# Block 3's attention output by seven products, with norms, unpacking and the weighing of q placed elsewhere

## The chip, the cores and the metric

The kernel runs on one core of one Trainium2 chip. The metric is the device time of one execution in microseconds. TensorE (PE) multiplies, and its results land in PSUM banks. VectorE (DVE) and ScalarE (ACT) read those banks; GpSimd (POOL) works on SBUF alone. SyncE (SP) issues most of the DMAs. Each engine runs its own queue in order, and waits on semaphores of the others.

## The reference, cut to what matters

A two-layer network over 2 x 1024 rows of 512 floats: linear attention, an FFN with 4-bit weights, gated linear attention, and an FFN over picked rows, each with a residual and a layernorm. The change lies in the first part alone:

```python
q = _feature_map(proj(Wq))          # elu(x) + 1
k = _feature_map(proj(Wk))
v = proj(Wv)
kv = jnp.einsum('bhtd,bhte->bhde', k, v)
z = 1.0 / (jnp.einsum('bhtd,bhd->bht', q, k.sum(axis=2)) + 1e-06)
out = jnp.einsum('bhtd,bhde,bht->bhte', q, kv, z)
...
x = _layernorm(x + out @ Wo.T)
```

## The kernel before

The 2048 rows are four blocks of 512 rows (0 and 1 are the first sequence, 2 and 3 the second), each held as four tiles of 128 x 512. In the first stage, which ends at about 236 us, a sequence `b` has blocks `i = 2b` and `j = 2b + 1`. The projections k and q of a block are Strassen's products in Winograd's form (`by_seven`): seven products of four 128x256 matmuls in place of sixteen 128x512 ones, for which DVE forms sums of the operands (S1, S2, S3 in lines 398 to 415) and adds results up. `elu1` (ACT lines 345 and 346, then DVE line 347) makes the feature map. POOL sums the rows of k (`sum_k`, line 461, one addition per tile); `add_xk` multiplies x and k on PE (line 442). One matmul with ones spreads the sum of k over the partitions (`ksumb`, line 467, copied by ACT in line 468). `weigh` (lines 483 to 489, DVE alone) divides each q row by its dot product with that sum, in five instructions per tile. PE then turns q (`turned`, line 235, copied by ACT in line 551).

The attention's output is q times a 512x512 matrix G (`G_rows`). For blocks 0, 1 and 2, `o_products` makes it of seven products (line 565), whose results DVE adds to x at once (line 571). Two of the products' operands, S1 and S2, come from `q_sums` (lines 519 and 520), two more from lines 582 and 587. Its last step takes the block's row statistics on DVE (`row_stats`, lines 226 and 227) and normalises the block: the power on POOL (line 219), and four POOL instructions (line 221). Block 3's output is made tile by tile instead (`add_o`, line 610): four 128x512 matmuls, an addition to x (line 617) and the tile's statistics, with the turning of the next tile between.

The FFN's packed weights are unpacked in the background: `unpack_some(n)` takes n jobs, each a load on SP into one of two buffers (line 285), a shift and a mask on DVE (lines 288 and 289), and one or two copies on ACT (line 292). There are 16 jobs of 704 columns and 11 of 512.

The order is made by hand: `run` takes the steps of a list of products and, behind each, the other steps listed for it. `behind()` chains PE's instructions in that order, `tc.issue_after` puts an instruction behind another, and a scheduler orders what is free.

PSUM has eight banks. `acc_bank` takes banks 4 to 7 in turn, and the FFN stage takes its first banks by where that turn stands:

```python
last = turn_of["acc"]
y_banks = [4 + (last + i) % 4 for i in (2, 3, 0, 1)]
chunk_banks = [(2, 3), (0, 1), tuple(y_banks[2:])]
```

The FFN stage begins with three chunks side by side. Each step of a chunk is two 128x512 matmuls (line 942) into its `gatep` or `upp` bank, scaled in place by ACT (line 967) or DVE (line 969) ahead of the next step. Block 0's input for it is split into `x1Th` and `x1Tl` in lines 267 and 268. Some of these matmuls are scheduled between block 3's products.

Of the kernel before, what the change touches and what calls it, by code (L numbers as in the profile page):

```python
# [10 lines left out]
F32 = mybir.dt.float32  # L11
# [5 lines left out]
ALU = mybir.AluOpType  # L17
AX = mybir.AxisListType
# [3 lines left out]
P = 128  # L22
B, T, C = 2, 1024, 512
NB = 4
KC = C // P
# [48 lines left out]
def body(ctx: ExitStack, tc: tile.TileContext, a: dict, out: bass.AP):  # L74
    nc = tc.nc
# [5 lines left out]
    sp = ctx.enter_context(tc.tile_pool(name="small", bufs=3))  # L81
# [14 lines left out]
    def acc_bank(name):  # L96
        return bank("acc", name)
# [43 lines left out]
    x_t = [x[:, :, :C] for x in x_row]  # L141
# [22 lines left out]
    t, src = new_xT(0)  # L164
# [59 lines left out]
    def row_stats(mv, x):  # L224
        st = sp.tile([P, 6], F32, tag="st", name="st")
        nc.vector.bn_stats(st, x)  # L226
        nc.vector.bn_aggr(mv, st)
# [80 lines left out]
    anchor = [None]  # L308
# [49 lines left out]
    for _ in range(7):  # L358
        ins = nc.tensor.matmul(idle[:, :P], ones, ones, start=True, stop=True).ins
    last_pe = [ins]  # L360

    def behind():

        return ExitStack() if last_pe[0] is None else tc.issue_after(last_pe[0])
# [67 lines left out]
    pairs_of, mv_of, G_of, acc_of, ksum_of = {}, {}, {}, {}, {}  # L432
    tile_of = lambda i: slice(i * P, (i + 1) * P)
# [44 lines left out]
    def weigh(blk, t):  # L478

        for r in range(2):  # L480
            x = pairs_of["q", blk][t][:, r]
            e = wk.tile([P, C], F32, tag="e", name="qk")
            nc.vector.tensor_mul(e, x, ksum_of[blk // 2])
            z = sp.tile([P, 16], F32, tag="z", name="z", bufs=2)
            nc.vector.tensor_reduce(z, e.rearrange("p (h d) -> p h d", d=32), AX.X, ALU.add)
            nc.vector.tensor_scalar_add(z, z, 1e-6)
            nc.vector.reciprocal(z, z)
            x3 = x.rearrange("p (h d) -> p h d", d=32)
            weighed[0] = nc.vector.tensor_mul(x3, x3, z.unsqueeze(2).to_broadcast([P, 16, 32])).ins

    weighed = [None]
    vkm_of, qT, TG, o_of, parts = {}, {}, {}, {}, []

    def values(b):
# [58 lines left out]
    def o_products(blk):  # L553

        A11, A12, A21, A22 = (qT[blk][:, 2 * e : 2 * e + 2, 256 * t : 256 * t + 256] for t in range(2) for e in range(2))
        G = G_of[blk // 2]
        B11, _, B21, B22 = (G[:, 2 * e : 2 * e + 2, 256 * o : 256 * o + 256] for e in range(2) for o in range(2))
        T1, T2, T3, T4 = TG[blk // 2]

        def product(ps, a, b, first, t, o):  # L560

            with behind():
                for r in range(2):
                    for k in range(2):
                        ins = nc.tensor.matmul(
                            ps[:, 256 * r : 256 * r + 256], a[:, k, r * P : (r + 1) * P], b[:, k],
                            start=first and r == 0 and k == 0, stop=k == 1, skip_group_check=True,
                        ).ins
            last_pe[0] = ins
            x = x_t[blk][:, 2 * t : 2 * t + 2, 256 * o : 256 * o + 256]  # L570
            return nc.vector.tensor_add(x, x, ps.rearrange("p (r c) -> p r c", r=2)).ins

        if blk not in S_of:
            q_sums(blk)
        S1, S2 = S_of[blk]
        grow = acc_bank("grow")
        added = product(grow, A11, B11, True, 0, 0)
        with tc.issue_after(added):
            for rest in TG_rest:
                rest()  # L580
            TG_rest.clear()
            nc.vector.tensor_sub(A21, A11, A21)
        yield
        product(acc_bank("P2"), A12, B21, True, 0, 0)
        yield
        product(grow, S2, T2, False, 1, 0)
        nc.vector.tensor_sub(A12, A12, S2)
        yield
        side = acc_bank("P7")
        product(side, A21, T3, True, 1, 1)  # L590
        yield
        product(grow, S1, T1, False, 1, 1)
        yield
        product(side, A22, T4, False, 1, 0)
        yield
        product(grow, A12, B22, False, 0, 1)
        yield
        mv = mv_of[blk] = sp.tile([P, 4, 2], F32, tag="mv", name="mv")
        with tc.issue_after(weighed[0]):
            for i in range(4):  # L600
                row_stats(mv[:, i], x_t[blk][:, i])
            layernorm(x_t[blk], mv, by=nc.gpsimd)
        yield

    def add_o(blk, i):

        ao = acc_bank("ao")
        with behind():
            for k in range(KC):
                ins = nc.tensor.matmul(  # L610
                    ao, qT[blk][:, k, tile_of(i)], G_of[blk // 2][:, k], start=k == 0, stop=k == KC - 1
                ).ins
        last_pe[0] = ins
        x = x_t[blk][:, i]
        if i == 0:
            mv_of[blk] = sp.tile([P, 4, 2], F32, tag="mv", name="mv")
        nc.vector.tensor_add(x, ao, x)
        row_stats(mv_of[blk][:, i], x)

    def split_some(*part):  # L620
        if 0 in part:
# [10 lines left out]
    for k in range(KC):  # L632
        for i in range(4):
            for o in (slice(0, 256), slice(256, 512)) if k == 0 else (slice(0, 512),):
                with behind():
                    last_pe[0] = nc.tensor.matmul(
                        first[i][:, o], xT[0][:, k, tile_of(i)], Wk[:, k, o],
                        start=k == 0 and o.start == 0, stop=k == KC - 1, skip_group_check=True,
# [21 lines left out]
    def some_xk(blk, *part):  # L660
        return [lambda i=i: add_xk(blk, i) for i in part]

    def turns(blk, *part):
        return [lambda i=i: turned(blk, i) for i in part]

    def some_o(blk, n):

        def one():
            if blk not in o_of:
                o_of[blk] = o_products(blk)  # L670
            next(o_of[blk])

        return [one] * n

    def whole_o(*part):
        return [lambda i=i: add_o(3, i) for i in part]

    job = lambda n: [lambda: unpack_some(n)]

    def k_products(blk):  # L680
        return by_seven(xT[blk], Wk, Ts["k"], S_rooms, pairs_of.setdefault(("k", blk), []), lambda t: sum_k(blk, t))

    def q_products(blk, ready):
        return by_seven(xT[blk], Wq, Ts["q"], S_rooms, pairs_of.setdefault(("q", blk), []), ready)

    step = lambda f, *x: [lambda: f(*x)]
# [4 lines left out]
    for b in range(B):  # L691
        i, j = 2 * b, 2 * b + 1
        if b:
            run(
                k_products(i),
                turns(1, 0, 1) + job(1), job(1),
                turns(1, 2, 3) + some_o(1, 1) + job(1), some_o(1, 2) + job(1), some_o(1, 5) + job(1),
            )
        q_ready = [] if b else step(q_weights)
        run(  # L700
            k_products(j), [],
            some_xk(i, 0, 1) + job(2), some_xk(i, 2) + job(1) + q_ready, some_xk(i, 3) + job(1), job(1 + b),
        )
        if b == 0:
            Ts["q"] = sums_of_weights(Wq, slices(staged[0], 0, 3))
        else:

            Tq = place_w(1, "Tq")
            for n in range(3):
                nc.scalar.copy(Tq[:, n], staged[0][:, n])  # L710
            Ts["q"] = (*slices(Tq, 0, 2), Ts["q"][2], *slices(Tq, 2, 3))
            S_rooms[0] = pieces_of(Tq[:, 3])
        run(
            q_products(i, lambda t: weigh(i, t)), [],
            some_xk(j, 0, 1) + job(1 + b), some_xk(j, 2) + step(spread_ksum, b) + job(1), some_xk(j, 3) + job(1 + b),
        )
        if b == 0:
            xT[2] = load_xT(2)
        split = [step(split_some, n) if b else [] for n in range(4)]
        rings["free"] = (rings["sum"][(turn_of["sum"] + 1) % 2],)  # L720
        run(
            q_products(j, lambda t: None),
            step(values, b),
            turns(i, 0, 1) + split[0] + job(1 - b),
            turns(i, 2, 3) + split[1] + step(q_sums, i) + step(G_rows, b),
            some_o(i, 2) + split[2] + some_o(i, 1) + job(1 - b),
            step(all_free) + some_o(i, 1) + step(weigh, j, 0) + split[3] + some_o(i, 3) + step(weigh, j, 1) + some_o(i, 1)
            + job(1 - b),
        )
        if b == 0:  # L730
            xT[3] = load_xT(3)
    for more in (
        turns(3, 0, 1) + whole_o(0) + turns(3, 2) + whole_o(1) + turns(3, 3) + whole_o(2, 3)
    ):
        more()
    late = mv_of[3]
# [186 lines left out]
    with tc.tile_pool(name="s2", bufs=1) as wk2:  # L923
# [24 lines left out]
        class Chunk:  # L948
# [29 lines left out]
            def step(self, e, k, by):  # L978
                self.product(e, k)
                self.end(e, k, by)  # L980

        class Normed:
# [35 lines left out]
            def stats(self, i):  # L1018
                row_stats(self.mv[:, i], x_t[self.blk][:, i])

            def norm(self, i):
                norm_tiles(self.blk, self.mv, (i,))
# [588 lines left out]
    turns, last_hp = [0], [None]  # L1611
# [436 lines left out]
```

## Time and profile before

| | |
|---|---|
| time, three runs | 906.47, 905.47, 903.45 us; median 905.47 us |
| the profiled execution | 904.14 us, span 902.4 us |
| mean granted TensorE clock | 0.998 |
| PE busy | 881.0 us, 98% of the span |
| DVE, ACT, POOL busy | 686.4, 378.9 and 262.1 us |

The span runs from the first to the last instruction of the profiled execution, whose own time is 1.74 us longer. The profile counts a float32 matmul as two records, so "x8" of 128x256 is one product of four matmuls. A row's first two numbers in the timeline are its start and its length; where several like it follow each other, they are merged. "L571" is line 571 of the kernel. What stands in brackets at the end is the idle time before it and what ended it.

### The profile page before, as it was taken

What the parts mean: (1) busy time and instruction counts of PE and PEld (TensorE: products, weight loads), DVE (VectorE), ACT (ScalarE), POOL (GpSimd) and SP (SyncE); (2) the same over time, 40 slices, a digit from 0 to 9 for tenths busy, and PEclk for the clock granted to TensorE, in tenths of its full rate; (3) what the DMA queues carried; (4) which work ended last, traced back from release to release, by engine and by line L of the source; (5) the groups of instructions that cost most, each with busy time, mean ns of one, the idle gap of its engine ahead of it and who ended that gap; (6) DMA issues with size and microseconds to landing.
All of it is one profiled execution on the core that took longest, in us unless ns stands there. A gap on an engine that the chain in (4) does not pass through costs nothing. (4 is left out here: it accounts for less than half of the span.)

```text
span 902.4 us, 10909 instructions
## 1 busy us (share of the span) xinstructions
PE 881.0 (98%) x3923; PEld 687.5 (76%) x3923; DVE 686.4 (76%) x1320; ACT 378.9 (42%) x648; POOL 262.1 (29%) x229
## 2 busy tenths in 40 slices
PE   9999999999999999999999989999999999999996
PEld 5668886687688888888876767787585888888886
DVE  2569995589787797897878975858977976998535
ACT  2345343463477886986866233231201223220000
POOL 1020075200573456655654220020340030000112
PEclk9999999999999999999999999999999999999999
DMA  9632211201421404314003144000024220330001
GB/s 319 225 98 79 77 62 47 92 26 24 118 82 48 47 1 99 43 58 117 13 24 97 44 94 187 1 1 0 1 95 142 92 94 1 115 119 1 12 36 47
DMA packets 88007, 64.85 MB, mean 72 GB/s; under 512 B 63214, under 2 KB 63770, under 8 KB 87441
## 3 DMA queue, kind: packets, MB, share of 16 engines
q1 hardware_dynamic: 85313, 58.89, 22.4%
q0 software_dynamic: 1920, 4.22, 1.2%
q10 hardware_dynamic: 720, 1.05, 0.3%
q8 instruction: 31, 0.51, 0.2%
q14 instruction: 23, 0.19, 0.1%
HBM read 48.37 MB, written 17.88 MB: 73 GB/s over the span
## 5 line engine op out<-in xcount | busy, mean ns | idle before, releaser
L1001 DVE TENSOR_TENSOR yp<-yp,ratio 128x512 f32<-128x512 f32 x160 | 103.3, 692 | 17.2 <-PE yp L942 16.8
L219 POOL TENSOR_TENSOR rs<-rs,table 128x4 f32<-128x4 f32 (+1 forms) x19 | 17.2, 904 | 292.0 <-DVE rs L218 291.8
L967 ACT ACTIVATE gatep<-gatep,scale 128x512 f32<-128x512 f32 x132 | 83.8, 658 | 35.9 <-PE gatep L942 26.5
L942 PE MATMUL gatep<-x1Th,wgu 128*128 128x512 f32 x176 | 70.2, 399 | 0.0
L942 PE MATMUL yp<-wdn,hhi 128*128 128x512 f32 x176 | 70.1, 398 | 0.0
L942 PE MATMUL yp<-wdn,hlo 128*128 128x512 f32 x176 | 69.9, 397 | 0.2 <-POOL hlo L976 0.2
L942 PE MATMUL gatep<-x1Tl,wgu 128*128 128x512 f32 x176 | 69.3, 394 | 0.3 <-DVE x1Tl L268 0.3
L942 PE MATMUL upp<-x1Tl,wgu 128*128 128x512 f32 x176 | 68.8, 391 | 0.0
L942 PE MATMUL upp<-x1Th,wgu 128*128 128x512 f32 x176 | 68.8, 391 | 0.0
L967 ACT ACTIVATE upp<-upp,scale 128x512 f32<-128x512 f32 x100 | 64.8, 663 | 6.5 <-PE upp L942 3.0
L976 POOL TENSOR_TENSOR hlo<-whole,hhi 128x512 fp32r<-128x512 f32 x43 | 55.6, 1292 | 3.5
L975 POOL CAST hhi<-whole 128x512 fp32r<-128x512 f32 x43 | 26.3, 611 | 88.4 <-DVE whole L973 86.9
L973 DVE SCALAR_TENSOR_TENSOR whole<-upp,scale,silu 128x512 f32<-128x512 f32 x43 | 32.3, 750 | 19.5 <-PE upp L942 11.4
L910 PE MATMUL go<-spare,spare 128*128 128x256 f32 x192 | 44.0, 381 | 0.0
L442 PE MATMUL xk<-pair,x 128*128 128x512 f32 x96 | 42.7, 592 | 0.0
L226 DVE BATCH_NORM_STATS2 st<-x 128x6 f32<-128x512 f32 x64 | 42.2, 674 | 0.4
L910 PEld LDWEIGHTS go<-spare,spare 128*128 128x128 f32 x192 | 36.0, 190 | 6.7 <-issue 2.1
L942 PEld LDWEIGHTS yp<-wdn,hhi 128*128 128x128 f32 x176 | 33.0, 188 | 9.6 <-DVE yp L1001 1.1
L942 PEld LDWEIGHTS gatep<-x1Th,wgu 128*128 128x128 f32 x176 | 33.0, 188 | 9.1 <-ACT gatep L967 1.1
L942 PEld LDWEIGHTS gatep<-x1Tl,wgu 128*128 128x128 f32 x176 | 33.1, 188 | 8.2 <-DVE x1Tl L268 0.6
L942 PEld LDWEIGHTS yp<-wdn,hlo 128*128 128x128 f32 x176 | 33.1, 188 | 8.0 <-POOL hlo L976 0.6
L1364 POOL TENSOR_TENSOR sum<-sum,sq 128x512 f32<-128x512 f32 x12 | 17.6, 1466 | 73.9 <-issue 63.9
(469 smaller groups left out, 2083.3 us busy)
## 6 DMA issues: line engine op xcount, KB each, us to landing
pk<-in_gu SPq DMA_DIRECT2D x16, 352.0 KB, 3.7
x<-in_x SPq DMA_DIRECT2D x4, 1024.0 KB, 14.1
w<-in_w SPq DMA_DIRECT2D x1, 4096.0 KB, 13.6
xs<-picked SPq DMA_DIRECT2D x4, 1024.0 KB, 4.9
out<-x SPq DMA_DIRECT2D x4, 1024.0 KB, 4.4
w<-in_w SPq DMA_DIRECT2D x4, 1024.0 KB, 7.4
x0T<-in_xT SPq DMA_DIRECT2D x3, 1024.0 KB, 7.5
x1r<-x SPq DMA_DIRECT2D x3, 1024.0 KB, 5.1
```

Source lines behind the costliest of these rows:

```text
L219: power = nc.gpsimd.tensor_tensor(rs[:, :n], rs[:, :n], const("mhalf")[:, :n], ALU.pow).ins
L226: nc.vector.bn_stats(st, x)
L442: ins = nc.tensor.matmul(acc_of[b][c], x_t[blk][:, i, c * P : (c + 1) * P], pairs_of["k", blk][i // 2][:, i % 2], start=blk % 2 == 0 and i ...
L910: ins = nc.tensor.matmul(ps[:, 256 * m : 256 * m + 256], w[:, k, m], b[:, k, 256 * half : 256 * half + 256], start=first and m == 0 and k ...
L942: nc.tensor.matmul(ps, w, x, start=start and n == 0, stop=stop and n == 1, skip_group_check=True)
L967: nc.scalar.activation(ps, ps, AF.Copy, scale=s)
L973: nc.vector.scalar_tensor_tensor(self.whole, ps, s, self.silu, ALU.mult, ALU.mult)
L975: nc.gpsimd.tensor_copy(hi, self.whole)
L976: nc.gpsimd.tensor_sub(lo, self.whole, hi.bitcast(F32))
L1001: nc.vector.tensor_tensor(self.y[:, i] if g == NI - 1 else ps, ps, ratio[:, g], ALU.mult)
L1364: nc.gpsimd.tensor_add(sum2, sum2, sq)
```

## The change

`o_products` also makes block 3's output, so `add_o` and `whole_o` go; block 3's four tiles of q are turned first, then come the seven products, then the statistics of its four tiles (`stats`). The end of `o_products` becomes a function `norm`, called for block 0 beside the last k products of block 3, for block 1 beside the q products of block 2, for block 2 where it was. Unpacking jobs beside the k products of block 2 fall from five to one, and rise from six to nine beside block 3's k products and from five to six beside block 2's q products. The weighing of q of blocks 1 and 3 is put behind the last two additions to x that precede it, and its second half is moved by one product.

```diff
-            weighed[0] = nc.vector.tensor_mul(x3, x3, z.unsqueeze(2).to_broadcast([P, 16, 32])).ins
-
-    weighed = [None]
+            with tc.issue_after(adds[-2 + r]) if blk % 2 else contextlib.nullcontext():
+                nc.vector.tensor_mul(e, x, ksum_of[blk // 2])
+                ...
+                weighed[0] = nc.vector.tensor_mul(x3, x3, z.unsqueeze(2).to_broadcast([P, 16, 32])).ins
+
+    weighed, adds = [None], []
...
-            return nc.vector.tensor_add(x, x, ps.rearrange("p (r c) -> p r c", r=2)).ins
+            adds.append(nc.vector.tensor_add(x, x, ps.rearrange("p (r c) -> p r c", r=2)).ins)
+            return adds[-1]
...
         product(grow, A12, B22, False, 0, 1)
         yield
+
+    def norm(blk):
+
         mv = mv_of[blk] = sp.tile([P, 4, 2], F32, tag="mv", name="mv")
-        with tc.issue_after(weighed[0]):
+        with tc.issue_after(anchor[0] if blk < 2 else weighed[0]):
             for i in range(4):
                 row_stats(mv[:, i], x_t[blk][:, i])
             layernorm(x_t[blk], mv, by=nc.gpsimd)
-        yield
-
-    def add_o(blk, i):
-        ...
+
+    def stats(blk):
+
+        mv_of[blk] = sp.tile([P, 4, 2], F32, tag="mv", name="mv")
+        for i in range(4):
+            row_stats(mv_of[blk][:, i], x_t[blk][:, i])
...
                 k_products(i),
-                turns(1, 0, 1) + job(1), job(1),
-                turns(1, 2, 3) + some_o(1, 1) + job(1), some_o(1, 2) + job(1), some_o(1, 5) + job(1),
+                [], turns(1, 0, 1),
+                turns(1, 2, 3) + some_o(1, 1), some_o(1, 2), some_o(1, 4) + job(1),
...
-            k_products(j), [],
-            some_xk(i, 0, 1) + job(2), some_xk(i, 2) + job(1) + q_ready, some_xk(i, 3) + job(1), job(1 + b),
+            k_products(j), job(b),
+            some_xk(i, 0, 1) + job(2), some_xk(i, 2) + job(1 + b) + q_ready,
+            some_xk(i, 3) + (step(norm, 0) if b else []) + job(1 + b), job(1 + b),
...
-            q_products(i, lambda t: weigh(i, t)), [],
-            some_xk(j, 0, 1) + job(1 + b), ...
+            q_products(i, lambda t: weigh(i, t)), job(b),
+            some_xk(j, 0, 1) + (step(norm, 1) if b else []) + job(1 + b), ...
...
-            step(all_free) + some_o(i, 1) + step(weigh, j, 0) + split[3] + some_o(i, 3) + step(weigh, j, 1) + some_o(i, 1)
-            + job(1 - b),
+            step(all_free) + some_o(i, 1) + split[3] + some_o(i, 1) + step(weigh, j, 0) + some_o(i, 2) + step(weigh, j, 1)
+            + (step(norm, i) if b else []) + job(1 - b),
...
-        turns(3, 0, 1) + whole_o(0) + turns(3, 2) + whole_o(1) + turns(3, 3) + whole_o(2, 3)
+        turns(3, 0, 1, 2, 3) + some_o(3, 7) + step(stats, 3)
```

In the changed program PE's instructions after block 2's last product stand in this order: four FFN matmuls, the turning of block 3's tile 0, four FFN matmuls, the turning of tiles 1, 2 and 3, two products, two FFN matmuls, five products, and the FFN.

More of the change, by code (lines that the diff above doesn't have):

```diff
@@ L482, in weigh @@
             e = wk.tile([P, C], F32, tag="e", name="qk")
-            nc.vector.tensor_mul(e, x, ksum_of[blk // 2])
             z = sp.tile([P, 16], F32, tag="z", name="z", bufs=2)
[L485 to L489, printed above, removed]
-    weighed = [None]
+            with tc.issue_after(adds[-2 + r]) if blk % 2 else contextlib.nullcontext():
+                nc.vector.tensor_mul(e, x, ksum_of[blk // 2])
+                nc.vector.tensor_reduce(z, e.rearrange("p (h d) -> p h d", d=32), AX.X, ALU.add)
+                nc.vector.tensor_scalar_add(z, z, 1e-6)
+                nc.vector.reciprocal(z, z)
+                x3 = x.rearrange("p (h d) -> p h d", d=32)
+                weighed[0] = nc.vector.tensor_mul(x3, x3, z.unsqueeze(2).to_broadcast([P, 16, 32])).ins
+    weighed, adds = [None], []
     vkm_of, qT, TG, o_of, parts = {}, {}, {}, {}, []
@@ L602, in o_products @@
             layernorm(x_t[blk], mv, by=nc.gpsimd)
-        yield
-    def add_o(blk, i):
[L607 to L618, printed above, removed]
+    def stats(blk):
+        mv_of[blk] = sp.tile([P, 4, 2], F32, tag="mv", name="mv")
+        for i in range(4):
+            row_stats(mv_of[blk][:, i], x_t[blk][:, i])
     def split_some(*part):
@@ L673, in some_o @@
         return [one] * n
-    def whole_o(*part):
-        return [lambda i=i: add_o(3, i) for i in part]
     job = lambda n: [lambda: unpack_some(n)]
@@ L713, in body @@
         run(
-            q_products(i, lambda t: weigh(i, t)), [],
-            some_xk(j, 0, 1) + job(1 + b), some_xk(j, 2) + step(spread_ksum, b) + job(1), some_xk(j, 3) + job(1 + b),
+            q_products(i, lambda t: weigh(i, t)), job(b),
+            some_xk(j, 0, 1) + (step(norm, 1) if b else []) + job(1 + b), some_xk(j, 2) + step(spread_ksum, b) + job(1), some_xk(j, 3) + job(1 + b),
         )
```

## Prediction

> **What bounds the kernel now.** I read the page's first section, the waits of PE, and then the first stage (to 236 us) in the timelines of PE, DVE and POOL.
>
> ```profile
> PE 881.0 (98%) x3923; PEld 687.5 (76%) x3923; DVE 686.4 (76%) x1320; ACT 378.9 (42%) x648; POOL 262.1 (29%) x229
> ```
>
> PE is the bound: a change gains by taking work from PE or by ending one of its waits, and loses by adding a wait. The granted clock is 0.998, so the clock is no matter here. PE's waits that touch the edited lines are few:
>
> ```profile
> PE grow L565 <- DVE x L571: 1.5, 2, 0.8
> ...
> PE grow L565 <- DVE qS L520: 0.6, 1, 0.6
> PE P L565 <- DVE x L571: 0.4, 1, 0.4
> PE gatep L942 <- DVE x1Tl L268: 0.3, 1, 0.3
> ```
>
> The timeline puts the first three rows at 100 to 131 us (0.38, 0.68, 0.55 and 0.82, together 2.43 us). All are waits for DVE, which is busy 34.72 of the 35 us from 98 to 133. The fourth is at 217 us. So 2.7 us at most is there to be won from waits. Of PE I use these rows:
>
> ```profile
> 207.45 1.89 PE L391 MATMUL grow<-Wq,rw 128*128 128x256 f32 x8
> 214.79 1.89 PE L565 MATMUL P<-TG,qT 128*128 128x256 f32 x8
> 216.52 0.24 PE L746 MATMUL pg<-table,sg 88*128 88x88 f32 x1
> ...
> 221.68 3.60 PE L610 MATMUL ao<-G,qT 128*128 128x512 f32 x8
> 225.12 0.60 PE L235 MATMUL qTp<-table,pair 128*128 128x128 f32 x4
> 225.56 3.60 PE L610 MATMUL ao<-G,qT 128*128 128x512 f32 x8
> 228.99 0.60 PE L235 MATMUL qTp<-table,pair 128*128 128x128 f32 x4
> ```
>
> A product of four 128x256 matmuls takes 1.72 us from start to start (216.52 less 214.79), a tile of `add_o` 3.44 (225.12 less 221.68), a turning 0.44, an FFN matmul 0.23 (221.01 less 220.78). Of DVE, the weighing of block 3:
>
> ```profile
> 210.67 0.69 DVE L347 SCALAR_TENSOR_TENSOR pair<-grow,e 128x512 f32<-128x512 f32 x1 [1.42 <-ACT e L346]
> ...
> 222.64 0.69 DVE L489 TENSOR_TENSOR pair<-pair,z 128x512 f32<-128x512 f32 x1
> ...
> 223.52 0.69 DVE L489 TENSOR_TENSOR pair<-pair,z 128x512 f32<-128x512 f32 x1
> ```
>
> From 210.67 to 224.2 DVE never idles. Now q's last two tiles are weighed at 223.3 and 224.2 but turned at 225.12 and 228.99: the tilewise products of the earlier tiles cover them.
>
> **Part 1, the products.** Four tiles of 3.44 (13.76) become seven products of 1.72 (12.04): -1.72 us of PE. DVE gains seven instructions of 0.60 each (two sums, two differences, three more additions to x), priced in part 4.
>
> **Part 2, 98 to 133 us.** The additions to x now stand ahead of the weighing, and statistics (2.7 us of DVE) and four unpackings leave: the waits of 0.38, 0.68 and 0.55 go, in full I think. The fourth does not. In the new order of DVE, two shifts (L288), whose loads landed long before, stand right ahead of the addition that PE's last product of block 1 waits for. In before's clock that product could start at 130.06; the addition of the product three before it starts about 126.9, L347 follows at 127.5, the shifts at 128.1. Alone they take 0.50 each, and the addition is done at 129.8, in time. But POOL now adds the rows of k exactly then (it starts when L347 of k's first pair is done, 125.9, takes 0.97 and 1.4, and waits at about 128.1 for k's second pair), and beside such additions the trace has:
>
> ```profile
> 130.54 2.77 POOL L461 TENSOR_TENSOR ksum<-ksum,pair 128x512 f32<-128x512 f32 x2 [0.69 <-DVE pair L347]
> ...
> 130.92 1.27 DVE L288 TENSOR_SCALAR pk<-pk,shift 128x704 int32<-128x704 int32 x1
> 132.23 1.47 DVE L289 TENSOR_SCALAR pk<-pk 128x704 int32<-128x704 int32 x1
> ```
>
> Alone these take 0.58 and 0.52. With 1.27 and 1.47 the addition ends at 131.5: a wait of 1.4. Bounds: 0, if the shifts miss POOL's additions; 2.5, if L347 is caught too (1.75 at 128.65). I take 1.4, the nearest row. Part 2: -2.43 + 1.4 = -1.0 (from -2.4 to +0.1).
>
> **Part 3, 133 to 198 us.** Norms and unpackings come here, where DVE is busy 42.88 of 65 us and PE waits nowhere. What they are put ahead of matters. On POOL, block 0's norm stands ahead of the additions of block 3's k. In before's clock its statistics end with two shifts at 159.0 (L347 done 155.4, 2.7 and 0.8); the power takes 1.05, the four L221 10.5, so POOL is free at 170.5. The additions (2.8 a pair) then end at 176.1, and the `ksumb` matmul that needs them starts at 175.91 now: +0.2.
>
> ```profile
> 139.64 10.49 POOL L221 TENSOR_SCALAR x<-x,mv,rs 128x512 f32<-128x512 f32 x4
> ```
>
> On DVE four unpacking instructions now fall beside those additions. Four such took 3.69 at 162.71 to 166.2, against 1.54 alone, so 2.15 more. The path: L347 at 168.39 plus 0.6, statistics 2.66, unpackings 3.69 end at 175.3; ACT's copy 0.63 frees the buffer, the next load takes 3.3, L288 and L289 0.85, then on ACT L292, L468 and L418 1.6: 181.8. The product of 181.93 that waits for L418 is just met, but DVE's next step, at 179.38 now, is 2.4 late, and the idle times up to the weighing of block 2 (0.60 and 0.96) give back 1.56. That weighing (L347 at 186.18 to 197.6 without a gap) has no slack: PE turns its last tile at 197.6. So +0.85, with `ksumb` +1.1. Bounds: 0, if the unpackings miss the additions; 3.2, if the four unpackings behind L418, which stand beside block 1's norm, lose 2.15 too. SP's queue keeps its order: the loads of unpacking issue later, and behind them only the store of block 1, whose readers wait for 218 us anyway, so it costs nothing; without that cover its 5 us would be seen.
>
> [...]
>
> **Part 4, 207 to 240 us.** In the changed order block 3's four tiles are turned ahead of all its products. Block 2's last product starts at 216.52 and ends at 218.24; eight FFN matmuls (1.84) and three turnings (1.32) later, at 221.4, PE wants the last tile. On DVE the same instructions run from 210.67 as before, but an addition now stands ahead of the second L347 and waits for the product of 210.90, done 212.6 plus 0.3 (as at 105.25, where an addition starts 0.3 after its product), while DVE is there at 211.9: +1.0. The last weighing thus ends at 225.2. PE waits 3.8, spread over three turnings, with everything of PE queued behind. It was 0 before. Below: 2.8, if that addition finds its product done. Above: 4.5, if L489's neighbours meet POOL.
>
> Then the sums S1 and S2 stand behind block 2's statistics: 225.2 + 2.7 + 0.6 + 0.6 + 0.1 + 0.7 = 229.9, against PE at 225.6 + 2 x 1.72 + 0.46 = 229.5: +0.3. The last addition to x frees the bank that the third chunk's `upp` takes, since `acc_bank`'s turn stands elsewhere: 0.3 + 0.68 = +1.0 of bare wait. Behind it DVE takes block 3's statistics (2.7) and a scaling (0.75) while PE has twelve FFN matmuls (2.8): +0.6. The wait for `x1Tl` (0.3) goes: `x1Tl` is early now. Part 4's waits: 3.8 + 0.3 + 1.0 + 0.6 - 0.3 = +5.4 (4.0 to 6.5). From there PE is dense, so what is lost stays lost.
>
> **Sum.** -1.72 - 1.0 + 1.1 + 5.4 = +3.8 us. The profiled execution took 904.14 (span 902.4): 907.9. The median of the runs is 1.33 higher: 909.3.
>
> **The rivals.** (a) The waits of part 4 stand but POOL and DVE do not meet, so parts 2 and 3 take their lower ends: -1.72 - 2.43 + 0 + 5.4 = +1.25, 906.7. For it: the placing was worked out to tenths. Against: the four POOL additions and the unpackings are ordered by the same L347s. (b) Not slower: DVE ends the weighing of block 3 by 221.4, where PE wants it, so the 3.8 goes: 909.3 - 3.8 = 905.5, and with (a) 903.0. It decides from 3.8 us earlier on, between L347 at 210.67 and the last L489; against it, 12.85 us of DVE stand there without a gap. With every wait gone it is -1.72 - 2.73 = -4.45, 901.0. (c) Both upper ends of parts 2 and 3: -1.72 + 0.1 + 3.2 + 5.4 = +7.0, 912.5. That the seven products are not run is excluded by the program's order.
>
> **How the numbers follow.** This kernel's runs spread over 3 us, so about 0.3% (2.7 us) is told from no change. My forecast, 909.3, has 0.50 and (c) 0.10, both slower: 0.60. (a) has 0.24, and is within. (b) has 0.16: 0.04 as priced (903.0 to 905.5), which is within, and 0.12 with nearly every wait gone (towards 901.0), which is faster. So same 0.28, faster 0.12. The range, 903.0 to 912.5, takes in (a), (c) and (b) as priced; it leaves out (b) with nearly every wait gone, and what lies above (c). The forecast's own range would be 908.2 to 911.5.
>
> **What would show it.** Right: PE's waits list L235 `qTp` behind L490 with 3 to 4 us, `upp` behind the addition of L572 with about 1 us; no L566 wait near 100 us. Wrong: turnings without idle time ahead of them, or PE's first FFN `yp` earlier than 246.3 us.

## The result and the profile after

The changed kernel takes 908.17 us (median of 10 executions, 906.99 to 909.42), the kernel before 905.59 (10 executions beside it): a ratio of 1.0029, 95% interval 1.002 to 1.0037. It is slower by 2.6 us; 3.8 had been forecast (909.3, against 905.47).

The profiled execution took 909.42 us (span 907.6), the longest of the ten, while that of before (904.14) was among the short ones. So the two profiles lie 5.3 us apart where the medians lie 2.6 apart; where the other 2.7 come from is taken up under "The sum and the medians".

I cut both timelines at PE instructions that every kernel here has: the first Strassen product of block 1 (19.4 us), the first `xk` product beside the k products of block 3 (136.3), the first `gp` product of the second sequence (198.7), the first `yp` of the FFN (246.3), the `lT` product (538.4) and the end of the span. The stretches, in us:

| kernel | to `xk` | to `gp` | to `yp` | to `lT` | to the end |
|---|---|---|---|---|---|
| before | 116.90 | 62.37 | 47.64 | 292.08 | 363.94 |
| changed | 114.21 | 65.77 | 52.04 | 292.17 | 363.95 |
| difference | -2.69 | +3.40 | +4.40 | +0.09 | +0.01 |

The change is won and lost in the first three stretches, which are the prediction's parts 2, 3 and 4 (part 1 lies in the third). In the list of waits of PE (what waited, for whom; us in total, times, longest) the rows that are new or that answer to those of before are these:

```profile
PE qTp L235 <- DVE pair L490: 4.1, 5, 2.0
...
PE upp L935 <- DVE x L572: 0.8, 1, 0.8
...
PE grow L391 <- ACT pair L418: 0.7, 1, 0.7
...
PE vk L502 <- DVE pair L426: 0.6, 1, 0.6
PE grow L566 <- DVE x L572: 0.5, 1, 0.5
PE upp L935 <- DVE upp L962: 0.3, 1, 0.3
```

Of the four waits at 98 to 133 us one is left (0.5). Two of the five turnings that wait are block 2's (0.62 and 0.65 near 197 us), three are block 3's. PE's timeline at these three:

```profile
221.99 0.63 PE L235 MATMUL qTp<-table,pair 128*128 128x128 f32 x4 [0.41 <-DVE pair L490]
224.60 0.66 PE L235 MATMUL qTp<-table,pair 128*128 128x128 f32 x4 [1.99 <-DVE pair L490]
225.73 1.11 PE L235 MATMUL qTp<-table,pair 128*128 128x128 f32 x4 [0.47 <-DVE pair L490]
226.63 2.94 PE L566 MATMUL grow<-G,qT 128*128 128x256 f32 x8
229.41 1.89 PE L566 MATMUL P<-G,qT 128*128 128x256 f32 x8
...
238.51 1.89 PE L566 MATMUL grow<-G,qT 128*128 128x256 f32 x8
241.18 0.50 PE L935 MATMUL upp<-x1Th,wgu 128*128 128x512 f32 x1 [0.78 <-DVE x L572]
```

They idle 2.87 us (0.41 + 1.99 + 0.47). The fourth turning and the product after it are slow by themselves: 1.11 and 2.94 us where such rows take 0.60 and 1.89. The reason is in the windows of one microsecond there (of a row's last three numbers the first is the granted clock):

```profile
225.00:226.00 1.00, 0.53 (x5) 0.29 (x4) 1.00 (x3) 0.59 (x1) 0.00 (x0) 0.66 0.00 0
226.00:227.00 1.00, 1.00 (x5) 0.97 (x5) 1.00 (x4) 0.12 (x1) 0.00 (x0) 0.50 0.00 0
227.00:228.00 1.00, 1.00 (x4) 0.76 (x3) 1.00 (x3) 0.46 (x1) 0.00 (x0) 0.50 0.06 16
228.00:229.00 1.00, 1.00 (x5) 0.80 (x4) 0.93 (x4) 0.00 (x0) 0.00 (x0) 0.63 0.00 0
```

The clock fell to half for 3.4 us ((0.34 + 0.50 + 0.50 + 0.37) / 0.5). Before, no window ahead of the last few microseconds was below 1. From the scale transposition `pg` to the first `yp` the changed kernel took 32.49 us; a later kernel with the same instructions and no such fall took 31.21 (`late_jobs` below): the fall cost 1.28.

### The profile page after: what moved, and what is told of

The parts are those of the page before. It is cut to its first block, busy times and chain, and to the rows that moved or that the text cites. A ratio compares the mean times of both kernels' runs of the same rounds, so it can differ in the third digit from the quotient of the medians.

```text
span 907.6 us, 10975 instructions
## 1 busy us (share of the span) xinstructions
PE 882.4 (97%) x3947; PEld 693.9 (76%) x3947; DVE 689.0 (76%) x1327; ACT 378.6 (42%) x648; POOL 259.4 (29%) x229
## 5 line engine op out<-in xcount | busy, mean ns | idle before, releaser
L935 PEld LDWEIGHTS upp<-x1Th,wgu 128*128 128x128 f32 x176 | 33.0, 188 | 9.2 <-DVE x L572 1.2
```

The costliest lines, as they stand in the source:

```text
L935: nc.tensor.matmul(ps, w, x, start=start and n == 0, stop=stop and n == 1, skip_group_check=True)
```

## The experiments

**The change in two halves.** `only_products` puts the seven products of block 3 into the kernel before; `only_placing` makes the same edit the other way round in the changed kernel.

```diff
-turns(3, 0, 1) + whole_o(0) + turns(3, 2) + whole_o(1) + turns(3, 3) + whole_o(2, 3)
+turns(3, 0, 1, 2, 3) + some_o(3, 7) + step(stats, 3)
```

> The kernel before with one part of the change alone: block 3's output by seven products, its four tiles turned first, its statistics last; norms, unpacking and weighing of q stay where they were. My theory (the loss is made at the turnings of block 3): this part alone is slower than before by 2.7 to 3.7 us (-1.72 for the products, +2.8 to 3.8 at the turnings, since the weighing here has no addition to x ahead of it, and +1.6 to 1.9 for S2, the third chunk's bank and the statistics), 908.3 to 909.3; PE's waits list turnings behind the weighing with 2 us or more. Rival (the loss comes from norms and unpackings beside POOL's additions, 133 to 198 us): within 0.5 us of before, 905.6, with turnings that wait less than 1 us in all.

> The changed kernel with block 3's output made tile by tile again as before; norms, unpacking and weighing of q stay at their new places. My theory: the waits at 98 to 133 us that go and those that come at 133 to 198 us cancel to within a microsecond: 905.7 to 906.3, no turning of block 3 waits, but the copy of line 418, the product of vk and the turnings of block 2 (near 180, 186 and 197 us) make PE wait 2 to 3 us together. Rival (placing is the loss): 908 or more, the whole of the measured difference.

Measured: the products alone 909.57 us, ratio to before 1.0045 (1.0028 to 1.0062); the placing alone 906.15, 1.001 (0.9997 to 1.0022). The halves by stretches:

| kernel | to `xk` | to `gp` | to `yp` |
|---|---|---|---|
| before | 116.90 | 62.37 | 47.64 |
| only_products | 116.94 | 62.36 | 51.58 |
| only_placing | 114.20 | 64.63 | 47.62 |

Each half moves its own stretches and leaves the others alone to 0.04 us. Not all was as expected: the products alone came out just above the 908.3 to 909.3 expected, with turnings that waited 1.8 us (1.54 + 0.23), not 2 or more; with the placing alone the turnings of block 2 waited 1.3, but neither the copy of line 418 nor `vk` made PE wait. The products make the third stretch 3.9 us longer (in an execution with a mean granted clock of 0.991, against 0.998 before), though they are 1.7 us less work for PE. The placing wins 2.7 and gives back 2.3. So the loss is at block 3, as forecast, and the placing is worth nothing that the times can tell. The two medians (+4.1 and +0.7) add up to more than the whole change (+2.6); with intervals of 1 to 1.5 us each that is not settled. Falls of the clock are one reason: none of the six executions with the products alone has a mean granted clock above 0.996, and the median ones have 0.994, which two profiles with two falls each show (`mix2_late`, `mix3`).

**The order at block 3.** `mix` turns two tiles, makes the two products that need only them, and then turns the rest.

```diff
-turns(3, 0, 1, 2, 3) + some_o(3, 7) + step(stats, 3)
+turns(3, 0, 1) + some_o(3, 2) + turns(3, 2, 3) + some_o(3, 5) + step(stats, 3)
```

> The changed kernel with block 3's order mended: tiles 0 and 1 are turned, then the two products that need them alone (A11 B11, A12 B21), then tiles 2 and 3, then the sums and the other five products; the third chunk's banks are ones that were free long before. My theory: the turnings' waits (3.4 us from start to start) fall to about 0.6, and the wait for the bank (0.9) goes; S2 stands behind block 2's statistics on DVE, so a new wait of about 2.4 us comes ahead of the product with S2. Sum -2 us against the changed kernel, 906.2; if PE's clock falls to half there no more, up to 1.3 us less in the profiled execution. Rival (DVE is the bound of this stretch, waits of PE only move): 908.2 as the changed kernel, with the new wait as long as those that went.

The waits came as expected. The turnings of block 3 kept one wait of 0.4, and in their place stood this row:

```profile
PE grow L566 <- DVE qS L521: 2.3, 1, 2.3
```

The third stretch took 50.41 us, against 52.04 with a fall of the clock and about 50.8 without. That is 0.4 us of true gain, not 2: DVE was late, and PE's wait moved from the turnings to the product that needs S2. The time was 910.27 (1.0058, 1.0044 to 1.0072), worse than the profile gives reason for: the profiled execution was, with 908.31, the shortest of the six, and what the other five met I did not see; three of them have a mean granted clock of 0.995, the profile 0.997. My 906.2 failed, and the rival (waits only move) is nearer.

**The bank.** `banks` takes the FFN's first banks two turns on.

```diff
-last = turn_of["acc"]
+last = turn_of["acc"] + 2
```

> The changed kernel with the FFN's first banks taken two turns on, so that the third chunk's gatep and upp take P2's and P7's banks rather than a turning's and grow's. My theory: the wait for the last addition to x (0.8 us idle, 0.9 from start to start) goes from the list, but the next one, for the scaling of upp behind block 3's statistics, grows by nearly the same, since DVE's order stays: 908.0, within 0.4 us of the changed kernel. Rival (the bank is worth its own wait): 1.0 us less, 907.1.

Measured 908.53 (1.0039, 1.0025 to 1.0053). The wait of `upp` for the addition in line 572 is gone; the one for the scaling in line 962 grew from 0.3 to 0.9 us, and the third stretch took 50.78 us, the 50.8 of the changed kernel without its fall. What PE is spared ahead of a DVE step that keeps its time is waited for at that step.

**Who gives back the early gain.** In the changed kernel the weighing of block 2 begins with a row of line 347 on DVE, which waits for ACT. ACT's timeline, and DVE's:

```profile
184.62 1.15 ACT L292 ACTIVATE wdn<-pk 128x512 fp32r<-128x512 f16 x2 [1.63 <-DVE pk L289]
185.68 0.58 ACT L345 ACTIVATE e<-grow 128x512 f32<-128x512 f32 x1
```

```profile
186.95 0.69 DVE L347 SCALAR_TENSOR_TENSOR pair<-grow,e 128x512 f32<-128x512 f32 x1 [0.83 <-ACT e L346]
```

Two copies of the unpacking (line 292) stand in ACT's queue ahead of line 345, and they wait for DVE to unpack. Before, the same row of line 347 came at 186.18, though PE was 2.6 us later there at 162 us. `late_jobs` puts these two jobs behind the weighing.

```diff
-some_xk(j, 3) + job(1 + b),
+some_xk(j, 3) + job(1 - b), step(jobs_behind, weighed, 2 * b),
```

> The changed kernel with two unpacking jobs put behind the weighing of block 2 (they stood ahead of it: their two copies on ACT come before line 345, which line 347 and with it the weighing wait for). My theory by now (the 2.7 us that PE wins before 133 us are given back because this weighing does not start earlier, held by these jobs): line 347 of that pair starts at about 183 us rather than 186, the turnings of block 2 near 196 us wait no more (1.6 us from start to start), vk neither (0.25): 1.9 us less than the changed kernel, 906.3. Rival (POOL's additions beside the unpackings are the loss, as the prediction had it): within 0.4 us of the changed kernel, 908.

Line 345 now ran at 182.22 and line 347 at 183.52, and no turning of block 2 waited. The second stretch took 62.60 us, against 64.5 to 64.6 in `only_placing`, `mix` and `banks` and 62.37 before: the 2 us were found. But the third stretch grew from 50.8 to 52.21. PE's timeline shows where:

```profile
197.72 1.55 PE L532 MATMUL gp<-Wo,vkm 32*32 32x512 f32 x16 [0.19 <-ACT qT L552]
```

The jobs' copies now stood on ACT ahead of the copies of line 552 that free the banks for `gp`. From `gp` to `pg` it was 21.00 us instead of 19.54 (`banks`), all of it in the `gp` rows: 2.75 us from the first of them to the next product, against 1.30. The time was 907.8 (1.0037, 1.0024 to 1.005), not 906.3, and the changed kernel's interval does not tell it apart. The theory held for the place, and the price came back three steps later.

**The collision with POOL.** `norm0_late` puts block 0's norm behind POOL's additions.

```diff
-some_xk(i, 3) + (step(norm, 0) if b else []) + job(1 + b), job(1 + b),
+some_xk(i, 3) + job(1 + b), job(1 + b) + (step(norm, 0) if b else []),
```

> The changed kernel with block 0's norm put behind POOL's additions of block 3's k, so that POOL adds at about 157 to 166 us as before, and the unpackings at 168 to 173 us run beside a norm rather than beside additions. The prediction's part 3 (this collision is the loss of that stretch): the turnings of block 2 wait 1.2 us less or not at all, 906 to 907. My theory by now (the unpackings ahead of line 347 set the weighing, and the collision is covered in most executions): within 0.4 us of the changed kernel, 908.2, the two turnings still waiting 0.6 us each; lines 288 and 289 take 0.4 to 0.5 us there instead of 1.4.

Both were wrong: 910.53 us (1.0064, 1.005 to 1.0078), and a second stretch of 66.35 us. POOL's additions began at 157.97 and met the two unpackings there instead (lines 288 and 289: 2.90 and 1.82 us for two each). The norm's statistics then stood on DVE ahead of line 408, which came at 166.92 instead of 163.30 (`banks`), and `vk` waited 1.4 us. Moving POOL's work moved the collision; the statistics cost by their place on DVE.

**DVE's queue at block 3.** `mix2` is `mix` with the sums ahead of block 2's statistics, the product with A11-A21 first of the last five, and block 3's statistics in the FFN stage. `mix2_late` adds the move of `late_jobs`.

```diff
+nc.vector.tensor_add(S1, A21, A22)
+nc.vector.tensor_sub(A21, A11, A21)
+sums_end[0] = nc.vector.tensor_sub(S2, S1, A11).ins
...
-    with tc.issue_after(anchor[0] if blk < 2 else weighed[0]):
+    with tc.issue_after(anchor[0] if blk < 2 else sums_end[0]):
...
+add(3, i // 2, lambda i=i: row_stats(late[:, i], x_t[3][:, i]))
```

> The interleaved order of block 3 again (two tiles turned, two products, two tiles turned, five products), and now DVE's order mended as well: the sums S1, A11-A21 and S2 stand ahead of block 2's statistics, the product with A11-A21 comes first of the five, and block 3's statistics go into the FFN stage behind its first twelve scalings. My theory (what is late at block 3 is DVE, so the gain comes only where DVE's queue is mended): the wait for S2 of 2.3 us falls to about 1, the one behind block 3's statistics (1.0) goes; from the gp product of block 2 to the first yp about 49.0 us, against 50.4 in the interleaved kernel and 50.8 in the one with other banks: 906.5. Rival (DVE has no room there whatever its order): as the changed kernel, 908.

> The interleaved order with DVE's queue mended and the two late unpacking jobs, together. If the two repairs lie at different places and add up, 1.9 and 1.7 us less than the changed kernel: 904.6, that is 1 us below the kernel before. If the second only takes what the first gives (one chain), as the better of the two, 906.3.

In `mix2` the third stretch fell to 48.20 us, as hoped. Yet the time was 910.95 (1.0071, 1.0058 to 1.0085), and the fourth stretch, which no kernel had moved so far, took 296.75 instead of 292.1. `mix2_late` was the same there, 297.10, in 909.94 us (1.0054, 1.004 to 1.0068); its third stretch was 49.67. In both, one `yp` product waited 1.8 and 2.4 us, and the clock fell to half behind it, at 252.0 and 254.2 us. I took the moved statistics for the cause and was wrong, as `mix3` showed.

**Jobs far down, and statistics spread.** In `placing_late` the two jobs stand behind the third product of block 2's output, in `only_placing`; `mix3` is `mix2` with the same move and the statistics of block 3 one tile per chunk (their normalising and the store of the block move down with them).

```diff
-some_xk(j, 3) + job(1 + b),
+some_xk(j, 3) + job(1 - b),
...
-some_o(i, 2) + split[2] + some_o(i, 1) + job(1 - b),
+some_o(i, 2) + split[2] + some_o(i, 1) + (step(jobs_behind_adds, 2) if b else job(1)),
```

> Norms, unpacking and weighing of q at the changed places, block 3 tile by tile as before, and the two unpacking jobs that held the weighing of block 2 moved far down: behind the third product of block 2's output, where ACT and DVE have idle time (near 207 to 211 us). My theory: the turnings of block 2 wait no more (-1.6), vk neither (-0.25), and this time nothing later waits for the jobs' copies: the gp product of block 2 follows block 2's first xk product by 62.6 us (64.6 without this move, 62.4 before), the first yp another 47.6 later. Sum: 2.7 us won before 133 us and kept but for 0.2: 2 to 2.5 us below the kernel before, about 903. Rival (the gain of the early stretch is always given back at the next DVE step): as with the placing alone, within 0.5 us of before.

> The interleaved order of block 3 with DVE's queue mended, block 3's statistics spread over four later chunks of the FFN (in the run before they stood in one place and made yp wait 1.8 us), and the two unpacking jobs moved far down. My theory: gp to first yp 48.2 us as there, no wait for yp above 0.5, block 2's stretch as in the placing kernel with the move; 906.2 from the yp row alone less 2: about 904, within 0.3% of before, with seven products against four tiles worth nothing: 1.7 us of PE won, 2.3 of waits that stay. Rival (the products pay once DVE is in order): 903 or less, and below the tilewise kernel of this call.

`placing_late` took 903.32 us, 0.9978 of before (0.9969 to 0.9987): faster than both kernels. Of PE's waits between 98 and 245 us these are left:

```profile
PE grow L391 <- ACT pair L418: 0.7, 1, 0.7
PE grow L566 <- DVE x L572: 0.5, 1, 0.5
PE qTp L235 <- DVE pair L490: 0.4, 1, 0.4
```

Its stretches are 114.21, 63.41 and 47.69. So the early gain can be kept, if what stands ahead of the next DVE step is moved with it.

`mix3` took 907.28 (1.0016, 1.0005 to 1.0027); the fourth stretch was 296.42. Spreading the statistics had changed nothing. DVE's timeline and the queue of SP name the cause:

```profile
249.93 3.69 DVE L1025 TENSOR_TENSOR yp<-yp,ratio 128x512 f32<-128x512 f32 x6 [3.58 <-DMA ratio<-steps]
```

```profile
241.27 0.37 SPq L246 DMA_DIRECT2D x1r<-x  x1
...
242.42 9.05 SPq L951 DMA_DIRECT2D ratio<-steps  x11
```

The store of block 2's rows (line 246) waits for block 2's norm, which I had moved down; behind it on SP's queue stand the loads of `ratio` that the first `yp` scaling needs. `mix4` issues that store behind them.

```diff
 put_rows(1, "x1r")
-put_rows(2, "x1r")
...
+add(8, 0, lambda: put_rows(2, "x1r"))
```

> As the kernel before this one in the list (interleaved order, DVE's queue mended, statistics of block 3 spread, two unpacking jobs far down), with the store of block 2's rows moved on SP's queue from ahead of the loads of ratio to behind them: in that kernel the store waited for block 2's norm until 241.3 us, the loads of ratio stood behind it, and the first yp scaling waited for the last of them until 249.9. My theory: the yp wait of 2.3 us goes with the clock's fall behind it (1.5); first yp at 245 us, as in the tilewise kernel with the move (245.02), so the seven products for block 3 are worth as much as the four tiles: 903 to 904. Rival (the products pay once their waits are gone): 902.3 or less. Second rival (another load or DVE step is late next): 905 or more.

903.9 us, 0.998 (0.997 to 0.999). The wait is gone, the fourth stretch is 292.20, the third 48.24. The tilewise kernel with the same move has 47.69 there and 903.32: with its waits repaired as far as I could, the seven products are worth no more than the four tiles. Their 1.7 us of PE are paid out again as 0.7 + 0.3 + 0.2 us of waits at block 3 and the restarts behind them. (A wait of 0.4 at a turning stands in both kernels.)

**The clock.** `filled` puts four matmuls of no use ahead of the third turning, into the bank that it overwrites.

```diff
+filled = acc_bank("qTp")
+for _ in range(4):
+    nc.tensor.matmul(filled, ones, G_of[1][:, 0], start=True, stop=True)
```

> The changed kernel with four 128x512 matmuls of no use put ahead of the third turning of block 3, into the bank that this turning overwrites, where PE waits 2.0 us anyway. Theory of the clock (PE's idle time at the turnings lets the granted clock fall to 0.5 for 3.4 us in some executions, which cost 1.3 us in the changed kernel's profile): the turning starts when it did, no window near 225 us has a clock below 1, and the median falls by 0.5 to 1, the share of executions in which it happened times 1.3. Rival (the fall has nothing to do with that idle time): it shows again in some runs, time unchanged or up to 1.7 us longer.

No window ahead of the end fell below 1 in its profile, and the third stretch was 50.78. The filling was longer than the wait, though: the third turning came 3.90 us behind the second, not 2.61 as in `banks`. And `banks` and `late_jobs` show no fall either without a filling (both profiles have a mean granted clock of 0.998, as has the one of before), and the time was 908.71 (1.0044, 1.0026 to 1.0061): no gain seen. As a test of time this is inconclusive; what decides whether the clock falls was not shown.

## Why the prediction was right or wrong

**The sign and the place were right.** PE is the bound, and four tiles of q turned ahead of all products wait for DVE: the turnings are listed behind line 490 and `upp` behind line 572, no wait is left near 100 us, and the first `yp` came at 251.5 us, all as named.

**Part 1, the products (-1.72).** Right: the last products start at 1.72 to 1.73 us from each other.

**Part 2 (-1.0 forecast, -2.7 measured, outside its -2.4 to +0.1).** Two terms were mis-sized. The gone waits were counted by their listed idle time, 2.43 us. From start to start they cost more: the product at 100.55 came 2.27 us after the one before, 0.55 over the usual 1.73 where 0.38 is listed, and the next one 0.1 late again. By that count the four cost 3.5, so a listed wait of half a microsecond cost about 0.3 more. The new wait was forecast at 1.4 and took 0.54. The mechanism was the one named: the shifts stand ahead of the addition and meet POOL's additions.

```profile
125.67 2.09 DVE L288 TENSOR_SCALAR pk<-pk,shift 128x704 int32<-128x704 int32 x2
127.68 0.67 DVE L572 TENSOR_TENSOR x<-x,grow 128x512 f32<-128x512 f32 x1
```

```profile
125.90 2.99 POOL L461 TENSOR_TENSOR ksum<-ksum,pair 128x512 f32<-128x512 f32 x2 [0.88 <-DVE pair L347]
```

They took 2.09 together, not 1.27 + 1.47. DVE came to them when forecast: PE's product ahead started 2.35 us earlier than before (125.99 against 128.34), so 125.67 is 128.0 in before's clock, against 128.1.

**Part 3 (+1.1 forecast; +3.4 in the profile, +2.1 to +2.3 in `only_placing`, `mix`, `banks` and `mix2`).** This step failed in its logic. I priced the lateness of block 2's weighing in before's clock (+0.85, in the changed profile line 347 is 0.77 later) and then added part 2's gain as if it were kept. But a weighing that does not start earlier takes back whatever PE has won until it arrives. The two parts are one sum, about +1 by my own rows and +0.7 in the profile. The holder I named, the collision of four unpackings with POOL, is the smaller part of it: line 347 came at 186.95 in the changed kernel and still at 185.92 in `banks`, where line 289 runs ahead of POOL. `late_jobs` (183.52) and `placing_late` show the larger one, the two jobs ahead of line 345. That I let the two jobs stand was the overlooked step.

**Part 4 (+5.4 of waits forecast).** The turnings were to wait 3.8, and idled 2.87 (3.4 from start to start). `upp` was to wait 1.0 and waited 0.78, the scaling behind block 3's statistics 0.6 and 0.31, S2 0.3 and nothing (0.40 in `banks`, where the clock did not fall and PE came earlier). So without the fall of the clock the third stretch is some 3.1 longer, against 3.7 forecast. The fall (1.28) had no term at all: the prediction had set the clock aside because before's profile shows 0.998.

**The sum and the medians.** -2.7 + 3.4 + 4.4 gives 5.1 of the 5.3 between the profiles. Take off the fall (1.28) and the worse case of part 3 (65.77 against 64.6, 1.2) and 2.6 is left, which is the difference of the medians. That the medians compare like with like is likely, not shown. The mean granted clock of each execution tells of falls: of the kernel before there are 72 executions beside the experiments, and the 22 at 0.998 or more took 903.1 to 904.9 us, the 50 below that 904.7 to 907.2. So before's profile (904.14, 0.998, no fall) is shorter than its median (905.59), and nine of the changed kernel's ten lie below 0.998 too; the one at 0.998 took 906.99. The 1.33 by which the forecast went from profile to median is then mostly the clock. The forecast of 3.8 came near in part by luck: the gain of part 2 was put 1.7 too small, the cost of part 3 about 1.1 too small and that of part 4 about 0.6 too large.

**The rivals.** (a), where POOL and DVE miss each other, is in part what some profiles show at line 289 (the last section). (b) needed DVE to be 3.8 us earlier at block 3; `mix2` to `mix4` show how far it can be brought, to a tie with the tiles.

## What to carry to other kernels

Time won ahead of a step that another engine holds is not won: before adding a gain up, follow PE to the next place where it needs that engine, and look at what stands ahead there in that engine's queue. A moved step takes its whole train along, its statistics on DVE, its store on SP's queue and the loads behind that store; here `late_jobs` and `mix2` found their microseconds and lost them at the next such place, and only `placing_late` and `mix4` kept them. And a wait listed with half a microsecond cost PE about 0.3 more here: the four at 98 to 133 us are listed with 2.43 us and cost 3.5 from start to start.

## What the runs showed of the hardware

**A few tenths of a microsecond decide a collision.** Line 289 at 167 us unpacks beside the first of POOL's four additions. In the changed kernel the addition began first (the first two rows), and in `banks` line 289 began first (the third):

```profile
167.41 5.42 POOL L461 TENSOR_TENSOR ksum<-ksum,pair 128x512 f32<-128x512 f32 x4
```

```profile
167.56 1.40 DVE L289 TENSOR_SCALAR pk<-pk 128x512 int32<-128x512 int32 x1
```

```profile
167.84 0.41 DVE L289 TENSOR_SCALAR pk<-pk 128x512 int32<-128x512 int32 x1
```

In `banks` POOL started at 167.85. In four profiles DVE came first by 0.01 to 0.04 us (`only_placing`, `mix`, `banks`, `mix2`): 0.41 each time, and line 418 made PE wait nowhere. (In `late_jobs`, 0.26 ahead, it took 0.57; in `mix4`, where POOL was 0.89 ahead, 0.82.) In five POOL came first by 0.12 to 0.16 (the changed kernel, `mix2_late`, `placing_late`, `mix3`, `filled`): 1.39 to 1.43, DVE waited about 1.2 us longer for the load behind it (1.79 to 1.96 in four of them, against 0.61 to 0.75 in the four profiles above), and PE waited 0.6 to 0.8 at line 418. In the changed kernel line 289 ended 0.28 us behind the addition (168.96 against 168.68). Why line 289 takes 1.0 us more there was not shown; what the rows show is how little sets the two groups apart: a start 0.12 us behind the addition rather than 0.01 ahead of it.

**The clock can fall in the middle of a kernel.** In the changed kernel it fell to half at 225.33 us for 3.41 us; of the 3.42 us ahead of that PE was busy for 1.28. Five kernels have block 3 turnings that wait one after another. Of the other four, `norm0_late` had such a fall from 225.5 to 228.9 us, and `only_products` has a mean granted clock of 0.991 in its profiled execution. `banks` and `late_jobs`, whose longest turning wait is 2.0 us as in the changed kernel, have a mean of 0.998, as before has. In `filled`, where the third turning does not wait, no window ahead of 902 us is below 1.

All three `yp` waits of 1.8 to 2.4 us had a fall behind them (`mix2` at 252.0 us, `mix2_late` at 254.2, `mix3` at 251.8), and `mix4`, without that wait, had none there. All fourteen profiles have PE's wait of 3.0 us at `lT`. In `mix2_late`, `mix3` and `mix4` the clock fell to half at the end of it, at 547.7, 545.3 and 540.4 us, for 3.4 us each time, and the last stretch took 365.5 us instead of 363.9 to 364.0. In before, the changed kernel, `norm0_late`, `mix2`, `placing_late` and `filled` it stayed at 1 there, behind the same wait. So in these profiles a fall in the middle came at or just behind a wait of PE, but the wait of 3.0 us came with a fall in some and without one in others; what decides was not shown.
